# Recurrent layers: state copies on another engine, a power in two halves, and token differences made by a transfer

## The chip, the core and the metric

The program runs on one core of one Trainium2 chip. The core has five engines that work at the same time, each through its own instructions in order: TensorE (PE in the profile; PEld is its loading of weights), VectorE (DVE), ScalarE (ACT), GpSimd (POOL) and SyncE (SP). They wait for one another by semaphores. Transfers are started by SP or by GpSimd, as instructions in the order of that engine, and are then carried out by 16 DMA engines. The metric is the time of one execution on the device, in microseconds; less is better.

## The reference

Four blocks run one after the other on x, of 4 sequences x 512 tokens x 512 channels: a grouped cross-attention (layer 0), two recurrent blocks with the same structure and other weights (layers 1 and 2), and a resampler with attention over 1024 positions and an MLP (layer 3). The change touches the recurrent blocks. Cut to what matters, one of them computes, with 32 heads of 16 channels:

```python
xa = _ln(x, ln1_w, ln1_b)
...
def step(s, inp):
    k_l, v_l, w_l, r_l = inp
    a = k_l[..., :, None] * v_l[..., None, :]
    out = einsum('bhs,bhst->bht', r_l, faaaa * a + s)
    return (a + w_l[..., None] * s, out)
...
y = ((y - gm) * rsqrt(gv + EPS)).reshape(B, L, C) * gn_w + gn_b
x = x + y * g @ Wo.T
xc = _ln(x, ln2_w, ln2_b)
sxc = concatenate([state[:, i0][:, None], xc[:, :-1]], axis=1) - xc
xk2 = xc + sxc * fmaa_k
xr2 = xc + sxc * fmaa_r
rr = sigmoid(xr2 @ fWr.T)
kk = square(relu(xk2 @ fWk.T))
x = x + rr * (kk @ fWv.T)
```

The three things to see are the state s that is handed from token to token, the inverse square root of each head's variance gv, and the difference sxc between a token's channels and those of the token before it. All values are float32.

## The kernel before

Each recurrent layer is cut into units of 256 tokens: two layers x four sequences x two halves make 16 units. In a unit the state is kept for all 32 heads as 8 groups g (a half e of the value channels and a key channel index i), and one group is one step of the program. A unit is thus 8 steps, and the whole recurrence is 128 steps, from about 776 to 2290 us. The order of every engine is written out by hand: the program runs over the steps g, and generators hang their pieces of work onto a step and one of four phases in it (EARLY, SOON, MID, LATE, in this order). `yield 12, LATE` means: go on in phase LATE of step 12 of this unit. Three generators belong to a unit: `mixes` (layer norm, token shift, the five mixed inputs and their products, from step -11 to 1), `outputs` (the head norm and the output product, steps 9 to 15) and `channels` (the channel mixing, steps 19 to 27). So one step carries work of up to three units. Nothing reorders the instructions afterwards: what is emitted first on an engine runs first on it.

A step g is emitted in this order. `summed(g-1)` puts the group sums of the last step (py) on TensorE. `begun(g+1)` prepares the next step: two VectorE products into the tiles kv (two buffers) and A (one buffer) (L833), a copy of the state into the first columns of kv (L839), the adding transfer kv<-A, which GpSimd starts (L584), and a ScalarE copy into W (L844). `scan(g)` runs the scan over kv on VectorE (L862), copies the end state of kv into S in units that begin a sequence (L864), and forms the products ry with r (L867). Then come the pieces of the four phases. In steps 2 and 6 of a unit TensorE spreads v out into the PSUM tile vr (L814), which L833 reads.

In `outputs`, the variance is brought into gn_rs (128x64) by VectorE (L927), raised to the power -1/2 by GpSimd with the constant tile mhalf (L929, step 11 EARLY), and copied into rp by ScalarE (L933, step 12 LATE), from which TensorE forms pbc. Later ScalarE forms yg (L945), and GpSimd multiplies it by the gate (L952).

In `channels`, xc is the normed and transposed input. `shift` forms the token differences sxc on GpSimd (L588 for tokens 1 to 255, L589 for token 0). `shifted` then forms xk and xr: four ScalarE passes that scale sxc per channel (L990), and a transfer, started by GpSimd, that adds xc (L584). TensorE multiplies xk by L_fk in step 24 MID and xr by L_fr in step 25 MID. The helper `shift` serves the recurrence's own token shift too: there it forms sx, which VectorE needs for mixx (L623).

All transfers that add are started by GpSimd through the helper `added` and queue behind each other and behind GpSimd's computing.

## Time and profile before

| | |
|---|---|
| median of 3 executions | 3747.28 us (3745.63 to 3757.73) |
| the profiled execution | 3749.93 us |
| its span, first to last instruction | 3748.2 us |
| TensorE busy | 3561.1 us, 95% |
| VectorE busy | 2748.8 us, 73% |
| ScalarE busy | 1667.2 us, 44% |
| GpSimd busy | 1762.1 us, 47% |
| power L929 | 16 x 11648 ns |
| state copies L864 | 64 x 819 ns |
| differences L588, channel mixing | 16 x 2178 ns |
| mean granted clock of TensorE | 0.971 |

How to read it. The profile records when each instruction ran on its engine. A line in order of time has the start, the duration, the engine, the line of the code, the operation, the tile written and the tiles read with their shapes, how many instructions are merged into the line, and in brackets how long the engine was idle before and what ended that. A group adds up such lines. A busy share is taken over the whole span, through stages with different limits, so it does not say what a change in one stage is worth; for that one looks at which wait ends last in the stage. TensorE's matmuls are pipelined and their ends are modelled.

The page cuts the span into 40 slices; the recurrence covers slices 9 to 24:

```profile
PE   9999999998899999999999996999999999999989
...
DVE  6777777679988888888988884388856666667531
ACT  4776776533444444444444432233344334334421
POOL 4777777524444444444444444155533433444430
```

Each digit is the busy share of a slice in tenths.

### The profile page before, as it was taken

How to read it: one execution, taken by the hardware profiler on the slowest of the kernel's cores; microseconds unless marked ns; L12 is line 12 of the kernel's file. 1: busy time of each engine (PE TensorE's matmuls, PEld its weight loads, DVE VectorE, ACT ScalarE, POOL GpSimd, SP SyncE). 2: the span in 40 equal slices, each digit the busy share in tenths (PEclk: the TensorE clock that was granted, in tenths of full speed). 3: DMA queues.
4: the chain of work that ended last, by engine and by line, in shares of the span. 5: the costliest groups of instructions: out<-in, count | busy, mean ns of one | idle time of the engine just before them, and what ended most of it. 6: DMA issues, size and time to landing. Idle time of an engine off the chain costs nothing.

```text
span 3748.2 us, 52355 instructions
## 1 busy us (share of the span) xinstructions
PE 3561.1 (95%) x20544; PEld 1894.1 (51%) x20544; DVE 2748.8 (73%) x4665; ACT 1667.2 (44%) x2486; POOL 1762.1 (47%) x834
## 2 busy tenths in 40 slices
PE   9999999998899999999999996999999999999989
PEld 3333333365565656656556653544455444544446
DVE  6777777679988888888988884388856666667531
ACT  4776776533444444444444432233344334334421
POOL 4777777524444444444444444155533433444430
PEclk9999998999899999999999998999999999999999
DMA  4000000056577777777777775410022112121223
GB/s 153 24 12 23 12 9 20 24 142 136 136 174 177 167 178 180 171 167 175 177 169 176 168 183 125 118 35 15 26 82 79 60 56 96 60 71 35 96 96 123
DMA packets 188805, 386.66 MB, mean 103 GB/s; under 512 B 18128, under 2 KB 44880, under 8 KB 186512
## 3 DMA queue, kind: packets, MB, share of 16 engines
q1 hardware_dynamic: 150256, 251.72, 21.3%
q0 software_dynamic: 38304, 131.61, 19.0%
q8 instruction: 162, 2.65, 0.3%
q14 instruction: 83, 0.68, 0.1%
HBM read 247.50 MB, written 4.19 MB: 67 GB/s over the span
## 4 chain that ended last, share of the span: by engine, by line
PE 72%; DVE 12%; DMA 5%; issue 4%; POOL 3%; ACT 3%; SPq 0%; POOLq 0%; DVEq 0%; ACTq 0%
PE pm L73 10%; PE ph L73 6%; PE pv L73 6%; PE po L73 6%; DMA kv<-A 5%; PE psc L242 5%; PE pst L279 5%; PE pst L1186 4%; PE psc L1186 4%; PE po L1252 3%; PE po L304 3%; PE pr L73 3%; PE pk L73 3%; DVE ry L867 3%; DVE kv L862 2%
## 5 line engine op out<-in xcount | busy, mean ns | idle before, releaser
L1247 POOL TENSOR_TENSOR acc<-acc,aT 128x2048 f32<-128x2048 f32 x96 | 436.2, 4544 | 337.9 <-ACT aT L1242 219.9
L292 POOL TENSOR_TENSOR aT<-aT,nmT 128x1536 f32<-128x1536 f32 x124 | 428.6, 3460 | 207.6 <-ACT aT L290 184.3
L254 DVE CUSTOM_DVE_ANT_0 sc<-psc,nm 128x512 f32<-128x512 f32 x512 | 354.1, 692 | 147.0 <-PE psc L242 89.3
L1231 DVE TENSOR_TENSOR aT<-pst,mb 128x512 f32<-128x512 f32 x512 | 317.8, 683 | 162.7 <-PE pst L1186 162.7
L867 DVE TENSOR_TENSOR ry<-kv,o_r 128x1024 f32<-128x1024 f32 x256 | 352.0, 1416 | 3.5
L862 DVE TENSOR_TENSOR_SCAN kv<-W,kv 128x1032 f32<-128x1032 f32 x128 | 296.4, 2316 | 0.2 <-DMA kv<-A 0.2
L584 POOL DMA_DIRECT2D kv<-A x127 | 118.9, 936 | 367.6 <-DVE kv L839 364.5
L290 ACT COPY aT<-pst 128x512 f32<-128x512 f32 x372 | 196.6, 595 | 178.0 <-PE pst L279 177.5
L298 ACT ACTIVATE aT<-aT 128x2048 f32<-128x2048 f32 x128 | 246.7, 1929 | 5.3 <-POOL aT L292 4.6
L73 PE MATMUL ph<-nT,l_m 128*128 128x256 f32 x1024 | 238.1, 388 | 0.0
L73 PE MATMUL po<-l_m,hT 128*128 128x512 f32 x512 | 233.1, 601 | 0.0
L73 PEld LDWEIGHTS ph<-nT,l_m 128*128 128x128 f32 x1024 | 193.4, 193 | 64.4 <-issue 24.8
L1200 DVE CUSTOM_DVE_ANT_0 sc<-psc,zeros,mx 128x512 f32<-128x512 f32 x256 | 176.7, 747 | 57.8 <-PE psc L1186 48.7
L279 PE MATMUL pst<-q,km 32*128 32x512 f32 x1024 | 206.4, 641 | 9.5 <-DVE mxs L254 5.8
L833 DVE TENSOR_TENSOR A<-vr,o_k 128x1024 f32<-128x1024 f32 x128 | 155.8, 1217 | 73.5 <-DMA kv<-A 73.5
L1242 ACT ACTIVATE aT<-aT 128x2048 f32<-128x2048 f32 x64 | 122.3, 1911 | 191.6 <-DVE aT L1231 191.4
L1240 ACT ACTIVATE aT<-aT,mc 128x2048 f32<-128x2048 f32 x64 | 128.1, 2002 | 162.3 <-DVE aT L1231 156.1
L1200 DVE CUSTOM_DVE_ANT_0 sc<-psc,nm 128x512 f32<-128x512 f32 x256 | 161.1, 686 | 52.2 <-PE psc L1186 52.2
L242 PE MATMUL psc<-km,q 32*128 32x512 f32 x1024 | 198.6, 650 | 0.8 <-ACT q L223 0.8
L881 PE MATMUL py<-ry,k 128*32 128x512 f32 x1024 | 161.1, 631 | 39.3 <-DVE ry L867 26.4
L929 POOL TENSOR_TENSOR gn_rs<-gn_rs,mhalf 128x64 f32<-128x64 f32 x16 | 186.4, 11648 | 24.7 <-DVE gn_rs L927 24.7
L1186 PE MATMUL psc<-kT,q 32*128 32x512 f32 x1024 | 171.0, 646 | 12.3 <-DVE aT L1231 11.5
(265 smaller groups left out, 7012.9 us busy)
## 6 DMA issues: line engine op xcount, KB each, us to landing
l_m<-in_L_W SPq DMA_DIRECT2D x64, 1024.0 KB, 5.1
kv<-A POOLq DMA_DIRECT2D x127, 516.0 KB, 7.4
L_wk<-in_L_Wk SPq DMA_DIRECT2D x16, 1024.0 KB, 8.0
L_wr<-in_L_Wr SPq DMA_DIRECT2D x16, 1024.0 KB, 7.5
L_wv<-in_L_Wv SPq DMA_DIRECT2D x16, 1024.0 KB, 6.0
L_wg<-in_L_Wg SPq DMA_DIRECT2D x16, 1024.0 KB, 7.8
L_wo<-in_L_Wo SPq DMA_DIRECT2D x64, 256.0 KB, 7.5
L_fk<-in_L_fWk SPq DMA_DIRECT2D x16, 1024.0 KB, 8.7
```

What stands on the lines that cost most here:

```text
L73: nc.tensor.matmul(ps, lhsT, rhs, start=(i == 0), stop=(i == len(pairs) - 1))
L242: nc.tensor.matmul(psc, d["q"][g][rs, lt * P : (lt + 1) * P], d["km"][rs, a, :], start=True, stop=True, tile_position=(32 * r, 0),)
L254: nc.vector.tensor_tensor_reduce(sc, ps[r], d["nm"][lt], 1.0, -3.0e38, ALU.add, ALU.max, mxs[:, a, lt, c : c + 1])
L279: nc.tensor.matmul(pst, d["km"][rs, a, s * P : (s + 1) * P], d["q2", a][rs, :], start=True, stop=True, tile_position=(32 * r, 0),)
L292: nc.gpsimd.tensor_tensor(w[:, n:, :], w[:, n:, :], nmT[:, None, :].to_broadcast([P, NR - n, L]), ALU.add)
L298: nc.scalar.activation(w, w, AF.Exp)
L862: nc.vector.tensor_tensor_scan(flat(kv), flat(W[g % 2]), flat(kv), 0.0, ALU.mult, ALU.add)
L867: nc.vector.tensor_tensor(y, kv[:, 4 * h : 4 * h + 4, None, :TP].to_broadcast([P, 4, 2, TP]), d["r"][:, i].rearrange("p (o m) -> p o m", o ...
L1186: nc.tensor.matmul(psc, lhsT[rs], rhs[rs], start=True, stop=True, tile_position=(32 * r, 0))
L1200: nc.vector.tensor_tensor_reduce(sc, ps[r], d["nm"][a], 1.0, mx[:, 0, lt, r : r + 1] if a else 3.0e38, ALU.add, ALU.min, mx[:, a, lt, r : ...
L1231: nc.vector.tensor_tensor(w[:, r, :], ps[r], d["mb"][:, r, :], ALU.subtract)
L1247: nc.gpsimd.tensor_tensor(d["acc", m], d["acc", m], w, ALU.add)
```

## The change

It has three parts. The copy of the end state from kv into S moves from VectorE (L864) to ScalarE, and from right behind the scan to phase SOON of the same step. The power on the 128x64 tile becomes two powers of 128x32, the first in the old place (step 11 EARLY), the second in step 12 EARLY. In the channel mixing the differences are made in another way: ScalarE writes -xc into sxc, GpSimd adds the previous token's row to column 0, and a transfer that GpSimd starts adds xc, shifted by one token, to columns 1 to 255. The forming of xk moves from 23 EARLY to 23 MID and that of xr from 23 LATE to 24 EARLY. Results are the same, and so is TensorE's order of work.

```diff
+        def kept(dst, src):
+            nc.scalar.copy(dst, src)
+            yield from ()
...
             nc.vector.tensor_tensor_scan(flat(kv), flat(W[g % 2]), flat(kv), 0.0, ALU.mult, ALU.add)
             if units[q][2] == 0:
-                nc.vector.tensor_copy(states(q)[:, i, e], quarters(kv)[:, :, :, TP])
+                steps.setdefault((g, SOON), []).append((q, kept(states(q)[:, i, e], quarters(kv)[:, :, :, TP])))
...
             yield 11, EARLY
-            nc.gpsimd.tensor_tensor(rstd, rstd, mhalf[:, :NQ], ALU.pow)
+            nc.gpsimd.tensor_tensor(rstd[:, : NQ // 2], rstd[:, : NQ // 2], mhalf[:, : NQ // 2], ALU.pow)
+            yield 12, EARLY
+            nc.gpsimd.tensor_tensor(rstd[:, NQ // 2 :], rstd[:, NQ // 2 :], mhalf[:, : NQ // 2], ALU.pow)
             yield 12, LATE
...
             sx = mq.tile([P, KC, TS], F32, tag="sxc", name="sxc", bufs=1)
-            shift(sx, cur, stT[:, :, b, 0] if hf == 0 else st[q - 1]["lastc"])
+            nc.scalar.activation(flat(sx), flat(cur), AF.Copy, scale=-1.0)
+            before = stT[:, :, b, 0] if hf == 0 else st[q - 1]["lastc"]
+            nc.gpsimd.tensor_tensor(sx[:, :, 0], sx[:, :, 0], before, ALU.add)
+            added(sx[:, :, 1:], cur[:, :, : TS - 1])
...
-            yield 23, EARLY
+            yield 23, MID
             xk = shifted("xk", V_FK)
-            yield 23, LATE
+            yield 24, EARLY
             xr = shifted("xr", V_FR)
             yield 24, MID
```

## The prediction

> **What bounds the kernel now.** I read the table of stages first, one row per recurrent unit (its columns: stage, length, then busy time of PE, PEld, DVE, ACT and POOL, then clock and transfers); then what PE waits for between 1000 and 2200 us; then single engines in order of time around each wait.

> ```profile
> 1245.51:1344.43 98.92, 93.17 (x627) 59.01 (x627) 82.86 (x86) 44.11 (x88) 45.55 (x31) 0.98 0.74 171
> 1344.43:1439.96 95.53, 91.60 (x628) 58.21 (x627) 85.98 (x95) 44.09 (x88) 46.09 (x31) 1.00 0.81 187
> ...
> PE ptn L572 <- DVE o_g L717: 17.4, 11, 2.9
> PE vr L814 <- DVE A L833: 13.2, 7, 3.7
> PE pbc L73 <- ACT rp L933: 9.6, 13, 0.7
> ...
> PE py L881 <- DVE ry L867: 6.1, 8, 0.9
> ```

> TensorE is the bound: 92 to 93 of 95 to 99 us per unit. ScalarE and GpSimd are busy under half of it, so work added to them costs only through waits. TensorE loses 4 to 6 us per unit, and three of the waits (ptn, vr, py) are waits for VectorE late in the unit. Why it is late:

> ```profile
> 1275.07 0.85 POOL L584 DMA_DIRECT2D kv<-A  x1 [1.79 <-DVE kv L839]
> 1275.63 11.72 POOL L929 TENSOR_TENSOR gn_rs<-gn_rs,mhalf 128x64 f32<-128x64 f32 x1
> ...
> 1289.95 1.81 POOL L584 DMA_DIRECT2D x<-xr  x2
> 1291.11 1.53 POOL L584 DMA_DIRECT2D kv<-A  x1
> ...
> 1303.40 1.23 DVE L833 TENSOR_TENSOR A<-vr,o_k 128x1024 f32<-128x1024 f32 x1 [5.38 <-DMA kv<-A]
> ...
> 1314.64 2.09 PE L814 MATMUL vr<-o_v,vsel 32*128 32x512 f32 x8 [2.06 <-DVE A L833]
> ```

> The next adding transfer kv<-A was ready at 1286.4 (its state copy L839 ends there) but stood behind the power and the two transfers behind it; 4.7 us later it starts, VectorE waits 5.38 us to reuse A, and TensorE 2.06. [...]

> ```profile
> 1517.32 2.33 POOL L588 TENSOR_TENSOR sxc<-xc 128x1020 f32<-128x1020 f32 x1
> ...
> 1517.84 2.37 DVE L783 TENSOR_TENSOR o_k<-o_k,o_w 128x512 f32<-128x512 f32 x1
> ...
> 1520.86 0.66 PE L572 MATMUL ptn<-ident,z 128*128 128x128 f32 x4 [2.90 <-DVE o_g L717]
> ...
> 1427.94 2.22 POOL L588 TENSOR_TENSOR sx<-xa 128x1020 f32<-128x1020 f32 x1
> ...
> 1427.90 2.30 DVE L864 COPY S<-kv 128x8 f32<-128x8 f32 x1
> 1430.12 2.35 DVE L867 TENSOR_TENSOR ry<-kv,o_r 128x1024 f32<-128x1024 f32 x2
> ...
> 1431.38 2.19 PE L881 MATMUL py<-ry,k 128*32 128x512 f32 x8 [0.86 <-DVE ry L867]
> ```

> L783 takes 0.68 us elsewhere, the state copy 0.17; each is stretched to the end of a GpSimd instruction.

> **Part 1, the power in halves.** One form of 128x64 takes 11.72 us, the 128x1 form of L79 0.55; between them 0.177 us per column, so a half costs 0.55 + 31 x 0.177 = 6.0 us, and two cost 12.1. The first keeps its place; stats, the two x transfers and kv<-A come next, then the second half. In the unit at 1275: first half to 1281.7, rs_cx waits for VectorE until 1282.4, the x transfers go at about 1284, kv<-A at 1286.5 in place of 1291.1, the second half ends at 1293, long before L933 wants it (1302). mix_g stands behind it, but its product ends at 1296.8. In the unit at 1374 the gain is 3.3 us. So the wait of 1.5 to 6.3 us at A shrinks to 0 to 1.6. TensorE's vr stalls: 13.2 us waited, and four of the seven matmul groups run about 2.1 instead of 1.14 because they trickle in, so 17; I count 15.

> **Part 2, state copies on ScalarE.** 64 copies, 52.4 us on VectorE (819 ns mean, median 174). By starts, an unblocked copy advances VectorE by only 0.09 us: 64 x 0.09 = 6 us. [...] I take 6. On ScalarE a copy is some 0.2 us (L611, 128x4, takes that), 13 us in its gaps. New waits: the copy waits for its scan, and VectorE's L833 of the next step but one overwrites that kv, so it waits for ScalarE. I placed all eight copies of the unit at 1344. In six ScalarE passes the spot after the scan and before L833. In one L833 moves from 1361.5 to 1362.2. In one the copy stands behind L744 and L750 (to 1385.1), so L833 moves from 1381.65 to 1385.4 and A from 1385.7 to 1386.6; behind it VectorE has 2.3 us idle before L894, which covers it. Cost 0; uncovered, 0.9 us in 8 units.

> **Part 3, the differences by transfer.** [...] Added: a ScalarE pass of 128x1024 (1.06, as L750), in the idle stretch before L698; a 128x4 add (0.2); a transfer of 510 KB in 512 runs of 1020 bytes. Moved: xk behind that transfer's landing, xr past the next kv<-A. Now GpSimd's order is: sxc transfer, kv<-A, xk transfer, **then** L588 for sx, which mixx waits for. In the unit at 1344 the sxc transfer starts at 1421.7 (after yg). With L from start to landing: xk's four passes run 1421.7 + L to + 1.7, its transfer starts, sx follows 0.6 later and takes 2.4. mixx has its sx at 1426.4 + L.

> L is in no row. The same bytes in 128 rows: mix_w 4.6 us on an empty queue; queued behind others xk 6.3, kv<-A 7.4, xr 11.0. Two x transfers (256 rows, half as long) end 0.93 + 4.3 = 5.2 us after the first starts, so doubling the rows costs under 0.6 us; 512 rows stay under 4.6 + 3 x 0.6 = 6.4, and generating the rows, 0.85 us for 128, could add up to 2.5. [...] Ends 4.6 and 12.3 (kv<-A's longest); I take 7.4, the row of the same engine at the same load.

> Then sx is there at 1433.8, where mixx started before (1433.59). But sx no longer lies on the scan's heels: ry ends 1430.2, not 1432.4, py starts when L_wo ends (1430.5, not 1431.38) and runs 1.06, not 2.19: TensorE is 1.9 us earlier, mixx is still in time, and xk lands at 1430.9 + 6.3 = 1437.2 against a need at 1438. Nine units have this py stall: 17 us, I count 15. Every us of L above 7.7 gives one back. [...]

> **Start and tail.** From 776 to 1000 VectorE is the bound (49 of 50 us): parts 1 and 2 give 3. In the tail there is no slack. The kv<-A of 2257 comes 4.6 earlier, less 1.2 for the longer xk chain. At 2314.9 the second half now stands behind rs_cx and the x transfers, which end at 2327: power done at 2332.6, not 2325.4, and pbc at 2333.7, not 2329.15: +4.6. The last unit:

> ```profile
> 2401.16 1.88 POOL L588 TENSOR_TENSOR sxc<-xc 128x1020 f32<-128x1020 f32 x1 [8.44 <-PE psc L1186]
> ...
> 2405.24 0.88 POOL L584 DMA_DIRECT2D xk<-xc  x1 [2.04 <-ACT xk L990]
> ...
> 2409.91 1.62 PE L73 MATMUL pm<-xk,L_fk 128*128 128x256 f32 x3 [5.59 <-issue]
> ```

> TensorE already idles 5.59 us here; negation, add and an idle-queue transfer (5.5) put xk's start at 2410: +4.9. Tail: +6.

> **Sum.** 15 + 10 + 15 = 40 us of stalls; a stall that goes lets TensorE reach the next one (pbc 0.7, pmm 0.6, var 0.5 stay, and o_g still follows GpSimd's yg), and the clock is 0.98 in most units, so two thirds: -27. Start -3, tail +6: -24. The profiled execution took 3749.93 us around its span of 3748.2; the median is 2.65 below it: 3747.3 - 24 = **3723**.

> **Rivals.**
> - The sxc transfer decides, slower. L = 12.3, kv<-A's longest: mixx gets sx at 1438.7, TensorE starts pm<-mixx at 1439.1, not 1436.2, so +3.0 in 14 units = +42; parts 1 and 2 still give 15 + 3, the tail costs 9: +33, **3780**. It decides from L = 10 on. For it: transfers are at 0.99 of all engines from 1431 on, and 1020-byte runs occur nowhere. Against: at 1421 they are at 0.68 and GpSimd's queue is empty.
> - No change, **3745**: kv<-A lands late through the x transfers ahead of it (12.3 us from start to landing at 1291), whatever its start, and L is near 9.6, where part 3 gives nothing. Against: the unit at 1390 landed in 8.1 behind the same transfers.
> - All stalls go, **3705**: the 40 us whole.
> - The halves or copies are not moved: the built order shows both, and TensorE's order unchanged.

> **Numbers.** Forecast 0.45, all stalls 0.14, no change 0.2, transfer decides 0.21. Range 3690 to 3778. About 11 us (0.3%) is what can be told from no change: faster 0.58, same 0.2, slower 0.22.

> **What would show it.** Right: L929's successors near 6.0 us each, no wait over 2 us at A after the power, vr stalls gone, the sxc transfer landing in 6 to 8 us, ry at the unit's end near 2.35. Wrong: mixx or pm<-xk waiting for a transfer in the units, a landing over 10 us, or sxc's start holding GpSimd over 2 us.

## The result and the profile after

| | before | after |
|---|---|---|
| median | 3752.61 us (3745.63 to 3762.78, 12 runs) | 3736.03 us (3733.41 to 3742.99, 12 runs) |
| ratio, 95% interval | 1 | 0.9956 (0.9946 to 0.9966) |
| the profiled execution | 3749.93 us | 3735.52 us |
| its span | 3748.2 us | 3733.7 us |
| mean granted clock | 0.971 | 0.973 |
| TensorE busy | 3561.1 us | 3543.7 us |
| first product with xk, unit 11 | 2125.49 us | 2091.95 us |
| first product with xk, unit 15 | 2409.91 us | 2395.66 us |

The changed kernel is faster by 16.6 us, where 24 were forecast. The last two rows say more than the total: by the channel mixing of unit 11 it is 33.5 us ahead, by that of unit 15 only 14.3.

The table of stages of the changed kernel, for the units from 1231.72 and 1328.77 us (columns as before: stage, length, busy time of PE, PEld, DVE, ACT, POOL, then clock and transfers):

```profile
1231.72:1328.77 97.05, 92.46 (x626) 58.80 (x627) 81.42 (x86) 45.16 (x89) 42.13 (x32) 0.98 0.80 180
1328.77:1423.89 95.12, 90.79 (x627) 58.14 (x627) 80.92 (x87) 46.17 (x97) 41.07 (x32) 1.00 0.83 193
```

Nine of the eleven units between 1041 and 2092 us look like the second, at full clock and 95.1 to 95.4 us long. Before, two of eleven had full clock, and lengths went from 95.5 to 100. What TensorE waits for between 1000 and 2200 us (total, times, longest):

```profile
PE pm L73 <- ACT th L641: 10.7, 11, 1.2
...
PE ptn L572 <- DVE o_g L717: 7.7, 12, 1.2
PE pm L73 <- DMA xk<-xc: 7.3, 1, 7.3
...
PE pm L73 <- DVE mixx L623: 5.6, 11, 0.8
PE vr L814 <- DVE A L833: 2.1, 1, 2.1
```

The three stalls that the prediction named have gone or shrunk: vr from 13.2 to 2.1, py from 6.1 to nothing, ptn from 17.4 to 7.7. Two new rows stand in their place, mixx and th, with 16.3 us against the 26.9 that went, and a single wait of 7.3 us for xk. The last is the first unit of the tail. Here it is in order of time (the fields as before):

```profile
2169.48 1.30 POOL L584 DMA_DIRECT2D sxc<-xc  x1
...
2173.97 0.89 POOL L584 DMA_DIRECT2D kv<-A  x1 [3.19 <-DVE kv L839]
...
2181.19 0.85 POOL L584 DMA_DIRECT2D xk<-xc  x1 [6.33 <-ACT xk L999]
...
2189.46 9.13 PE L73 MATMUL pm<-xk,L_fk 128*128 128x256 f32 x32 [7.27 <-DMA xk<-xc]
```

From the start of the sxc transfer to that of the xk transfer lie 11.7 us, and 8.3 more to TensorE's start. In units 0 to 11 the token mixing of a later unit fills that time on TensorE; from unit 12 on there is none.

### The profile page after: what moved, and what is told of

Its sections match the earlier page's. It is cut to its first block, busy times and chain, and to the rows that moved or that the text cites. A ratio compares the mean times of both kernels' runs of the same rounds, so it can differ in the third digit from the quotient of the medians.

```text
span 3733.7 us, 52458 instructions
## 1 busy us (share of the span) xinstructions
PE 3543.7 (95%) x20544; PEld 1889.6 (51%) x20544; DVE 2702.5 (72%) x4601; ACT 1691.7 (45%) x2566; POOL 1711.8 (46%) x850
## 3 DMA queue, kind: packets, MB, share of 16 engines
q8 instruction: 162, 2.65, 0.3%
## 5 line engine op out<-in xcount | busy, mean ns | idle before, releaser
L871 DVE TENSOR_TENSOR ry<-kv,o_r 128x1024 f32<-128x1024 f32 x256 | 372.2, 1495 | 7.2 <-DVE kv L866 0.5
L584 POOL DMA_DIRECT2D kv<-A x127 | 111.8, 880 | 356.8 <-DVE kv L839 236.5
L73 PE MATMUL ph<-nT,l_m 128*128 128x256 f32 x1024 | 235.8, 385 | 0.0
L73 PE MATMUL po<-l_m,hT 128*128 128x512 f32 x512 | 233.1, 601 | 0.0
L73 PEld LDWEIGHTS ph<-nT,l_m 128*128 128x128 f32 x1024 | 191.6, 191 | 64.2 <-issue 24.8
L1195 PE MATMUL psc<-kT,q 32*128 32x512 f32 x1024 | 171.8, 645 | 12.3 <-DVE aT L1240 11.4
L1195 PE MATMUL pst<-q,kT 32*128 32x512 f32 x1024 | 182.8, 649 | 0.0
L1254 POOL TENSOR_TENSOR acc<-aT 128x2048 f32<-128x2048 f32 x16 | 72.5, 4530 | 234.6 <-ACT aT L1249 234.6
L833 DVE TENSOR_TENSOR kv<-vr,o_k 128x1024 f32<-128x1024 f32 x128 | 155.6, 1216 | 25.6 <-ACT S L857 25.4
```

The costliest lines, as they stand in the source:

```text
L73: nc.tensor.matmul(ps, lhsT, rhs, start=(i == 0), stop=(i == len(pairs) - 1))
L871: nc.vector.tensor_tensor(y, kv[:, 4 * h : 4 * h + 4, None, :TP].to_broadcast([P, 4, 2, TP]), d["r"][:, i].rearrange("p (o m) -> p o m", o ...
L1195: nc.tensor.matmul(psc, lhsT[rs], rhs[rs], start=True, stop=True, tile_position=(32 * r, 0))
```

## The experiments

All twelve runs are set beside the kernel before on the same chip. Its median was 3746.72 to 3752.61 us in these rounds, so kernels of different rounds are best compared by their ratios. The next table has the medians, the ratios, and how many of the eleven units between the channel mixings of units 0 and 11 ran at a clock of 1.00; then by how many us the first product with xk starts earlier than in the kernel before, in the units 0, 11, 12, 13, 14 and 15 (each from one profiled execution).

| kernel | median us | ratio (95%) | units at 1.00 | q=0 | 11 | 12 | 13 | 14 | 15 |
|---|---|---|---|---|---|---|---|---|---|
| before | 3746.72 to 3752.61 | 1 | 2 | 0 | 0 | 0 | 0 | 0 | 0 |
| after | 3736.03 | 0.9956 (0.9946, 0.9966) | 9 | 4.0 | 33.5 | 24.8 | 28.9 | 19.2 | 14.2 |
| only_pow | 3722.55 | 0.9916 (0.9900, 0.9932) | 10 | 2.0 | 31.0 | 31.3 | 36.9 | 27.7 | 26.0 |
| only_copy | 3739.42 | 0.9959 (0.9944, 0.9975) | 4 | 4.8 | 13.9 | 12.2 | 13.1 | 12.5 | 10.9 |
| only_shift | 3764.07 | 1.0028 (1.0018, 1.0038) | 2 | 0.1 | 4.7 | -1.8 | -5.2 | -12.0 | -19.8 |
| tail_shift | 3721.93 | 0.9916 (0.9901, 0.9932) | 7 | 7.2 | 34.6 | 34.5 | 41.5 | 35.5 | 33.9 |
| pow_copy | 3724.14 | 0.9927 (0.9911, 0.9944) | 9 | -1.0 | 26.6 | 26.5 | 32.6 | 26.6 | 26.3 |
| pow_copy_tail | 3714.27 | 0.9902 (0.9884, 0.9920) | 9 | 0.2 | 27.4 | 27.3 | 33.4 | 31.9 | 31.9 |
| pow_tail | 3716.70 | 0.9906 (0.9886, 0.9926) | 9 | 0.3 | 27.4 | 27.7 | 33.2 | 31.9 | 31.9 |
| all_tail | 3716.20 | 0.9904 (0.9883, 0.9924) | 8 | 3.5 | 30.4 | 28.7 | 35.5 | 34.1 | 34.1 |
| all_tail_sx | 3714.66 | 0.9902 (0.9882, 0.9922) | 8 | 3.0 | 32.3 | 32.2 | 38.1 | 36.7 | 36.7 |

### Each part alone: only_pow, only_copy, only_shift

Each is the kernel before with one part of the diff shown above, and nothing else of it.

> The kernel before with part 1 alone: the group norm's power in two halves, the second a group later. Theory A (the three parts add up as the prediction's sum has them): TensorE's waits vr <- A between 1000 and 2200 us fall from 13.2 to about 2, worth 12 to 16 us in the middle with the groups that trickled in; the start gives 2; in the tail the second half stands behind the x transfers and pbc starts 4.6 later. Net -10 us, ratio 0.997. Rival B (the stall only moves on to py, ptn and mixx, because VectorE is late for other reasons too): ratio 0.9990 to 1.0015, with vr gone but py and ptn waits larger by as much.

Measured: 0.9916, 29 us faster. Neither theory had the size; the direction is A's. The vr wait fell to 2.5 us as A has it, but the units gained three times what the prediction's sum gave. The stall did not move on, as B has it: py's waits rose from 6.1 to 9.1 us between 1000 and 2200 us, and ptn's fell from 17.4 to 9.2.

> The kernel before with part 2 alone: the 64 state copies on ScalarE. [...] Rival B (the stretched copies, 52 us on VectorE, were work on the path): -15 us or more, ratio 0.996 or less, and the py waits of TensorE gone. Rival C (VectorE's kv of the next step but one waits for the copy behind ScalarE's long passes, 25 us in all): +5 to +10 us.

Measured: 0.9959, 12 us faster, short of the 15 of B. The py waits stay (6.1 us before, 6.3 now between 1000 and 2200 us), so B's path is not it, and C does not show. VectorE is busy for 7.8 us less in the eleven units, twice the 4 us that some 44 copies at 0.09 make, but VectorE's waits for kv<-A fell from 58.3 us to 32.2, TensorE's for vr from 13.2 to 7.9, and four units ran at full clock in place of two. A small advance of VectorE decided here in some units whether a stall came at all. That it works by this and by nothing else is argued, not shown.

> The kernel before with part 3 alone: the channel mixing's differences by a negation on ScalarE and an adding transfer, xk and xr later. Theory A (the changed kernel's trace: the middle units gain the ptn and py stalls, about 25 us, and pay about 15 for mixx and fk behind sx; the four last units, without a following token mixing, pay the longer chain to xk with 7, 4, 5 and 5 us): net 0 to +12 us, ratio 1.000 to 1.003. Rival B (the prediction's own terms, -25 x 2/3 in the middle and +6 in the tail): -10 us, ratio 0.997.

Measured: 1.0028, 12.5 us slower. A holds, at its upper end. By unit 11 the part has gained 4.7 us, and the four last units cost 24.5. The kernel with this part alone, what TensorE waits for between 2200 and 2420 us:

```profile
PE pm L73 <- DMA xk<-xc: 22.9, 3, 10.2
```

In the kernel before, the same window has one such wait of 5.2 us and one of 5.6 us that no transfer is named for.

Alone, the parts come to -29.0, -12.1 and +12.5, in sum -28.6; together they are -16.6. So they overlap by 12, about what the copies give alone.

### Parts 1 and 2 together: pow_copy

> Parts 1 and 2 together, without the transfer: the changed kernel with the differences of the channel mixing left on GpSimd and xk, xr at their earlier places. Theory A (once the power is in halves, the middle units run at 95.4 us and only short waits are left, so that parts 1 and 2 remove the same waits and their gains, 29 and 12 us alone, do not add up; the transfer costs the changed kernel some 15 us in the tail): 3714 to 3722 us, ratio 0.990 to 0.992. Rival B (the two gains add up): 3708 to 3712, ratio 0.989. Rival C (the transfer is needed for the gain of the changed kernel's middle units): 3730 or more.

Measured: 3724.14 us, 0.9927 (0.9911 to 0.9944). The median lies 2 us above A's range, and B and C are out. Beside the power in halves the state copies' place is worth nothing that can be told: the intervals of only_pow and pow_copy overlap. Both parts make VectorE earlier at the same A.

### The tail: tail_shift, pow_copy_tail, pow_tail

In tail_shift, a branch in `channels` keeps the old way in the last four units:

```diff
+            if q >= 12:
+                shift(sx, cur, stT[:, :, b, 0] if hf == 0 else st[q - 1]["lastc"])
+            else:
                 nc.scalar.activation(flat(sx), flat(cur), AF.Copy, scale=-1.0)
...
-            yield 23, MID
+            yield 23, EARLY if q >= 12 else MID
             xk = shifted("xk", V_FK)
-            yield 24, EARLY
+            yield (23, LATE) if q >= 12 else (24, EARLY)
```

> The changed kernel, but with the subtraction on GpSimd and the earlier places of xk and xr in the last four units (q of 12 and above), where no token mixing of a later unit follows; units 0 to 11 as changed. Theory A (the transfer's landing is bare in the tail, about 20 us of the 34 gained by 2092 us are given back there): TensorE's waits pm <- xk at 2189, 2264, 2331 and 2395 fall from 7.3, 9.0, 0.9 and 10.1 to about 0, 5.2, 0 and 5.6; 3716 to 3722 us, ratio 0.991 to 0.993 to the kernel before. Rival B (in the tail something else sets the end, such as the weights of the next stage or the norm's power, so that TensorE's earlier fk is lost again): 3732 to 3737, ratio 0.995 to 0.996, with longer waits at pbc or before psc.

Measured: 3721.93 us, 14 us below the changed kernel; A. The wait at unit 12 is down to 0.3 us, that at unit 13 is gone altogether (A had 5.2 us there), and unit 15 keeps 33.9 us of the 34.6 of unit 11.

In pow_copy_tail and pow_tail the power of the last unit is whole:

```diff
+            if q >= 15:
+                nc.gpsimd.tensor_tensor(rstd, rstd, mhalf[:, :NQ], ALU.pow)
+            else:
                 nc.gpsimd.tensor_tensor(rstd[:, : NQ // 2], rstd[:, : NQ // 2], mhalf[:, : NQ // 2], ALU.pow)
                 yield 12, EARLY
```

> As the run with parts 1 and 2 alone, but in the last unit (q = 15) the power in one piece, so that its second half does not stand behind the x transfers. Theory A (pbc of the last unit waits 4.4 us for the second half and nothing later hides that): 3 to 5 us less than parts 1 and 2 alone, the wait at pbc gone. Rival B (the last unit's xk chain or the next stage's work absorbs it): within 1 us of it.

Measured: 9.9 us below pow_copy by the medians, 4.7 by the two spans. The ranges of the runs overlap (3718.74 to 3725.42 and 3710.66 to 3719.68), so the size lies between. The wait of 4.4 us at pbc is gone, and unit 14's gain rose by 5.3, as A has it; the rest of the medians' distance has no row.

> Part 1 alone, with the power of the last unit (q = 15) in one piece; state copies on VectorE, differences on GpSimd. Theory A (once the power is split, neither the state copies' place nor the transfer is worth anything): 3712 to 3719 us, ratio 0.989 to 0.991, as parts 1 and 2 with the same last unit. Rival B (the state copies on ScalarE are worth a few us even then): 4 or more us above that run, ratio over 0.9915.

Measured: 3716.70 us, within A's range and 2.4 us above pow_copy_tail, which is inside both intervals: A. One part of three, and one piece for the last unit, is as fast as anything else that was run.

### Does the transfer pay in the middle? all_tail, all_tail_sx

all_tail is tail_shift with the last unit's power whole. all_tail_sx moves xk in units 0 to 11 one phase on, so that GpSimd computes the token mixing's sx (L588) before it issues the xk transfer:

```diff
-            yield 23, EARLY if q >= 12 else MID
+            yield 23, EARLY if q >= 12 else LATE
             xk = shifted("xk", V_FK)
```

> The changed kernel, with the differences on GpSimd in units 12 to 15 and the power of unit 15 in one piece. Theory A (both losses of the tail are then gone, 14 and 5 us): 3712 to 3718 us, ratio 0.989 to 0.991, as far as without the transfer, since the transfer's gain in the middle (py) is paid back at mixx and th. Rival B (the middle units of 95.15 us against 95.4 and the start add up to a real gain of the transfer): 3708 or less.

Measured: 3716.20 us, A. With both losses of the tail gone the transfer's kernel equals the one without the transfer (pow_tail).

> The same, but in units 0 to 11 xk takes its place a phase later, so that GpSimd computes the token mixing's sx before it issues xk's transfer. Theory A (mixx and fk lose 1.3 us per unit only because sx stands behind xk, which waits for sxc's landing): the waits pm <- mixx and pm <- th go, xk's transfer starts when its ScalarE passes end as before; but sx lies on the scan's heels again, so py gets back up to 0.8 us: units of 94.6 to 95.3 us, 3706 to 3714 us. Rival B (py's stall returns whole and xk lands later): units of 95.4 or more, 3716 or more.

Measured: 3714.66 us, 0.7 above A's range and below B's. The mechanism is A's: mixx is gone from TensorE's waits, th fell from 7.7 to 2.0 us, and py came back with 1.9 us in 12 waits of at most 0.2. But TensorE waits 0.16 us for ry again at one py of a unit, and the eight products there take 2.19 us where all_tail has 1.06; TensorE is busy for 1013.0 us in the eleven units where all_tail has 1005.4. Five of eight units at full clock are 94.7 to 95.1 us long, below every unit of pow_tail at full clock, yet the total cannot be told from pow_tail, pow_copy_tail or all_tail. It is open whether the transfer, well placed, is worth 2 us; it isn't worth 10.

### What a stall costs: stall4, stall5, stall3

only_pow gained 29.0 us between the channel mixings of units 0 and 11 (1080.1 to 1051.1 us). TensorE's waits in that stretch fell by 16.7 us (57.8 to 41.1); its busy time fell by 12.5 (1021.7 to 1009.2) at the same work. Around the vr stall at 1314.64, already shown, the kernel before has these stretches (stretch, length, PE busy, clock, and two columns of transfers):

```profile
1309.00:1313.00 4.00, 3.58 (x20) 1.00 0.03 5
1313.00:1317.00 4.00, 2.36 (x10) 0.68 0.17 32
1317.00:1321.00 4.00, 4.00 (x60) 0.89 0.95 242
1321.00:1325.00 4.00, 4.00 (x81) 1.00 0.63 135
```

The clock is full up to the stall and low for some microseconds after it, and vr itself runs 2.09 us. The same place in only_pow, where A is in time, in order of time on TensorE:

```profile
1301.26 1.14 PE L814 MATMUL vr<-o_v,vsel 32*128 32x512 f32 x8
...
1302.33 1.09 PE L572 MATMUL ptn<-ident,z 128*128 128x128 f32 x8
```

To tell a cost of the clock from one of VectorE's lateness, the probes put stalls of chosen length into a kernel that has none there: only_pow, with A computed again in nine units (the same values). The probes take 3751.58 (stall3), 3755.92 (stall4) and 3780.28 us (stall5).

```diff
-            for half, dst in ((seconds, kv), (firsts, A)):
+            again = 4 if 2 <= q < 11 and (e, i) == (1, 3) else 0
+            for half, dst in ((seconds, kv), *[(firsts, A)] * (1 + again)):
```

> A probe of what a TensorE stall costs: part 1 alone, and in nine units (q = 2 to 10) VectorE computes A of the last group before the new vr five times instead of once (4 x 1.13 = 4.5 us more of VectorE, the same values), whose slack before TensorE is 2.9 us in the trace of part 1 alone. Theory A (a stall under 2 us leaves the granted clock at 1.00): vr stalls of about 1.6 us, units of 95.4 + 1.6 = 97.0 us with clock 1.00. Rival B (any stall brings the clock down): units of 98.5 or more, clock 0.98.

Measured: eight stalls of 2.15 us, not 1.6 (the ninth, behind the start, is 7.7), and units of 99.0 to 99.2 us in six of the eight, with clock 0.98. By theory A's own rule this is already a stall over 2 us: 95.4 + 2.15 leaves 1.6 us, and the 3.4 us after the stall run at 0.52 to 0.55 in the first four. In seven of the eight places the clock fell. In one (1713.56 us) it stayed at 1.00 after the same 2.15 us, and vr ran 1.14 us there.

> As the probe before, with A computed six times (5.65 us more of VectorE). Theory A (a stall over 2 us is followed by some 3.3 us at half clock, which costs another 1.65 us): vr stalls of about 2.75 us, the clock in the 4 us after them near 0.6, units of 95.4 + 2.75 + 1.65 = 99.8 us in most of the nine units, with clock 0.98. Rival B (the clock falls for another reason and the stall costs its own length only): units of 98.1 us with clock 1.00.

Measured: eight stalls of 3.40 us (and a first of 9.3), units of 102.2 to 102.4 us. That is 95.4 + 3.4 + 3.5, twice the loss beyond the stall that A gave. The table of short stretches of stall5, right after one stall:

```profile
1324.20:1327.60 3.40, 3.39 (x15) 0.50 0.57 116
1327.60:1331.00 3.40, 3.40 (x39) 0.59 0.31 58
1331.00:1334.40 3.40, 3.40 (x68) 1.00 0.02 5
```

By the trace's record of the clock, the half clock lasts 6.83 us here (from 1323.58, within the stall, to 1330.41), where it lasted 3.41 after 2.15 us. Not all of the 3.5 us is due to it: each of these eight units has a further 3.41 us at half clock some 40 us behind its stall (1364.54 to 1367.95 after this one). B (own length only, 98.1 us at clock 1.00) is out.

> The probe again, with A computed four times in nine units (3.4 us more of VectorE). The longer probes stalled TensorE by 2.15 and 3.40 us and their units took 99.1 and 102.3 us. Theory A (a stall of about 1 us costs its length and no clock): vr stalls of 0.9 us, units of 96.3 us with clock 1.00. Rival B (the cost beyond the length is not the clock's but that of VectorE's lateness further on in the unit): units of 97.5 or more with clock 1.00.

Measured: the vr stalls are 0.9 us, but neither theory's unit came out, because VectorE's delay also reached o_g, and TensorE waited 2.9 us at ptn. It answers another question. The table of stages of stall3, two units one after the other:

```profile
1344.54:1442.91 98.37, 91.65 (x627) 58.21 (x627) 90.31 (x98) 44.38 (x88) 44.59 (x32) 1.00 0.76 181
1442.91:1542.93 100.02, 93.90 (x627) 59.39 (x626) 89.97 (x89) 44.36 (x88) 46.01 (x32) 0.97 0.73 169
```

Both have the same stalls (0.9 us, then 2.9 to 3.0), and so have the six other probed units behind the start. In every second one the clock fell; against the 98.3 to 98.4 us of the others that costs 0.9 us, or 1.7 where it fell a second time in the unit. So the clock fell behind stalls of 2.15 us and of 2.9 to 3.0 us in some places and not in others, and their length alone did not decide. The units alternate in kind as well (89 and 97 to 98 VectorE instructions, since every second one begins a sequence and copies states), so this run alone does not say what does.

```profile
1610.88:1614.29 3.41, 1.34 (x10) 1.00 0.44 151
1614.29:1617.71 3.42, 3.34 (x14) 0.50 0.90 252
...
1709.86:1713.28 3.42, 1.54 (x11) 1.00 0.44 122
1713.28:1716.69 3.41, 3.13 (x36) 1.00 0.96 280
```

Both stalls are 2.15 us long. Of the first, all but 0.1 us lies in one step, and the next step runs at half clock. The second lies across the border of two steps (0.3 us of it in the next), TensorE is busy for 1.54 us of the first in place of 1.34, and the clock stays.

This holds beyond the probes. Between 1040 and 2125 us the clock fell 86 times in the fourteen traces. In 38 of these TensorE was busy for less than half of the step before; only four steps at full clock with so little work (0.45 to 0.50 busy) were not followed by a fall. Before the other 48 falls TensorE was busy for 0.83 to 0.85 of the step, and pmm (L654), products with only 32 rows, filled 0.68 to 0.79 of it. These falls came without a long stall: 44 of the 45 steps at full clock that pmm filled to 0.70 or more were followed by one. The only unit of only_pow at 0.98 is of this kind:

```profile
1437.74:1441.16 3.42, 2.92 (x19) 1.00 0.61 120
1441.16:1444.57 3.41, 3.41 (x6) 0.50 0.46 89
```

Why the clock fell behind steps that pmm filled is not shown; no run changed pmm.

## Why the prediction was right, and where it was not

The sign and the range held, and the total is off by 7 us, but two of the terms were wrong by some 20 us each in opposite directions. That they nearly cancel is luck.

**What bounds the kernel.** Right: TensorE bounds it, and vr, ptn and py were the stalls that parts 1 and 3 take away.

**Part 1.** The chain from the power to vr was right in each step. A half takes 6.4 to 6.5 us on the chip, against 6.0. VectorE's waits for kv<-A fell from 58.3 us to 17.0 in only_pow, the longest from 6.3 to 2.6; vr went from 13.2 to 2.5. The size was wrong: 10 us in the middle by the sum, with about 2 at the start; measured 29. Three terms failed.

The first is the reading of vr's products of 2.1 us as products that "trickle in". They ran at half clock, as stall4's one exception shows (the same stall, the clock at 1.00, 1.14 us).

The second is the factor of two thirds, for which I gave, among other things, that "the clock is 0.98 in most units". The low clock was no background to be taken off but for the most part a second cost of the same stalls: TensorE's busy time fell by 12.5 us on top of the 16.7 waited, and ten of eleven units ran at 1.00. Of the eleven falls of the clock in these units of the kernel before, three follow a stall at vr, four a stall of 2.7 to 2.9 us at ptn, and four a step filled by pmm. only_pow has one, of the last kind. So perhaps 5 us of the 29 (an estimate: three falls fewer, at half of 3.41 us each) are due to where the grid lay in these executions.

The third is ptn, the 10 of the sum, which I counted under part 3. No run shows this term as part 3's own; what the runs showed in its place is this. With part 1 alone, and sxc still on GpSimd, L783 takes 808 ns in the mean, where it took 1496, and between the channel mixings of units 0 and 11 ptn's waits fall from 17.4 to 6.2 us. With part 3 alone L783 still takes 1351 ns: at 1515.64 it stretches to 2.87 us beside GpSimd's yg (L952). So what shortened L783 is that VectorE comes to it earlier (5.5 us before ptn at 1499.54 in only_pow, 3.0 us before it at 1517.84 in the kernel before), and not that sxc's subtraction is gone.

**Part 2.** Most of the time that left the copies came back at ry: in only_copy L871 takes 1585 ns in the mean, where L867 took 1416, 43.5 us more in all, while 52.4 us of copies left VectorE. L833's new waits for the copy are the two that were placed (0.49 us and 3.65 to 3.87), covered as said. In the middle no gain was forecast, and beside part 1 none is seen (pow_copy). Alone it gave 12 us, which the sum had no way to find, since it priced VectorE's time and not the chance that a stall comes.

**Part 3.** The duration L was right: 7.8 us median (5.4 to 9.6), against 7.4. Its gains came too: py's products and waits fell from 109.0 us to 94.1 between units 0 and 11 in only_shift, which is the 15 counted, and ptn's wait from 17.4 to 8.6 (where part 1 alone has 9.2, so the two cannot both be counted). But a net gain of 11 us was forecast (two thirds of 25, less 1.2 and 4.9 in the tail), and 12.5 were lost. In the middle the step that failed is "TensorE is 1.9 us earlier, mixx is still in time". I compared mixx with its own start before, when TensorE began on it at 1436.2; 1.9 us earlier it needs it at 1434.3, and VectorE, with sx at 1433.8, has 1.67 us of mixx still to do. So py's gain is waited away at mixx and at th behind it. The place in the changed kernel, in order of time:

```profile
1418.72 1.67 DVE L623 SCALAR_TENSOR_TENSOR mixx<-sx,L_vec,xa 128x256 f32<-128x256 f32 x4 [2.93 <-POOL sx L589]
...
1419.27 1.99 PE L73 MATMUL pm<-mixx,L_w 128*128 128x256 f32 x8 [0.60 <-DVE mixx L623]
...
1423.89 7.14 PE L73 MATMUL pm<-xk,L_fk 128*128 128x256 f32 x32 [0.79 <-ACT th L641]
```

With sx ahead of the xk transfer (all_tail_sx) the wait for mixx goes and that for th falls to 2.0 us.

**Tail.** +6 was forecast, with +4.6 for pbc and +4.9 for the last unit. Both are there: pbc waits 4.4 us, and the last unit loses 5.0 (19.2 to 14.2). What was left out is the same chain in units 12 to 14: I priced it for the last unit alone and let 1.2 us stand for the others. It costs 7.3 us in unit 12, 3.8 more than before in unit 13 (9.0 against 5.2), and of unit 14's fall of 9.7 us 4.5 are pbc's later start, and only 0.9 a wait for xk. Some 4.1 more are half clock, which the prediction did not price, behind the pbc stall (0.50 from 2303 to 2309 us) and behind a wait of 2.81 us for yg (0.80 and 0.64 in the two stretches of 3 us from 2318): pbc, pv and the product with L_wo take 1.22, 5.51 and 8.83 us, where they took 0.59, 3.73 and 7.13. Between units 11 and 15 the changed kernel gives back 19.3 us in all.

**Rivals.** "The transfer decides" had the right suspect and the wrong place: L never came near 12.3, and yet the part costs time, in the tail and not at pm<-mixx. "No change" and "not moved" fell. "All stalls go" comes nearest to what the middle did: 33.5 us by unit 11. But its 3705 leaves out the tail: 40 us of stalls and 3 at the start, less the 6 of the tail, make 3710.

## What to carry to other kernels

When TensorE is the bound and its clock in a stage is below 1, read the clock in short stretches around each stall: here the clock fell for one or two steps of 3.41 us, so a fall cost up to 1.7 or 3.4 us of work on top of the stall. Whether it fell behind a stall went with how much of one step the stall took (38 of 86 falls came after a step that was less than half busy), and so with where the grid lay; one of eight equal stalls of 2.15 us left the clock at 1.00. A transfer in place of an engine's pass put its landing time into a chain (here 7.8 us in the median, for a pass of 2.18); count every unit in which no other work covers that chain, not only the last, and test each "in time" against the consumer's new start, not its old one. Run the parts of a change one by one, since one of three can carry it: here the power in halves with a whole one in the last unit (3716.70 us, ratio 0.9906) beats the three together (3736.03, 0.9956).

## What was not expected of the hardware

- The granted clock fell after stalls of TensorE as short as 2.06 us; the same stall of 2.15 us left it at 1.00 once in eight times, when it lay across two steps of the clock's grid. In the faster kernels one to four of eleven units ran below 1.00, with one exception (all_tail at 1042.97) right behind a step of 3.41 us that products with 32 rows filled.
- The adding transfer of 510 KB in 512 runs of 1020 bytes lands 7.8 us after its start in the median, while mix_w, 512 KB on an empty queue in 128 rows, takes 4.6. A profile with both on an empty queue was not taken, so how much is due to the rows and how much to the other traffic stays open.
